# A fixed margin on every handover in the planner of a six-stage perceiver kernel

## The chip, the cores and the metric

The kernel runs on one core of a Trainium2 chip. The metric is device time in microseconds (us) from the start to the end of one execution. TensorE is called PE here, VectorE DVE, ScalarE ACT, GpSimd POOL and SyncE SP; PEld is the weight load of PE. SP does nothing but issue transfers (DMAs).

## What is computed

Two layers work on 128 sequences of 32 tokens with 256 features. Each sequence has a context of 257 tokens. Cut to its steps:

```python
x = x + L0_xattn(layernorm(x), ctx)       # 16 heads of 16; q and k are rms-normed, softmax over 257 keys
x = x + L0_attn(layernorm(x))             # differential attention, 2 heads, 32 keys, rope
x = x + L0_ffn(layernorm(x))              # silu-gated, 704 hidden, weights quantised to NF4 and back
x = x + L1_xattn(layernorm(x), mask, ctx) # 32 heads of 8: masked self attention + tanh(gate) * attention to ctx
x = x + L1_attn(layernorm(x))             # 16 heads, causal
x = x + L1_ffn(layernorm(x))              # 8 gated experts of 256, all computed, weighted by a router
```

## The kernel before

**Units.** Four sequences make a unit of 128 rows, so there are 32 units `h` in each layer. The two feed-forward steps take units in pairs. Numbers that need more than 16 bits are held as a high and a low part (names that end in `l`: `Pl`, `fhl`, `kkl`, `al`): ACT writes or rounds the high part, DVE or POOL subtracts to get the low part, and PE multiplies both.

**Streams.** The work is written as generators, one for each step, and each runs over its units: `ctx_load` and `ctx_gen` (keys and values of the context, written to DRAM), `load_k` and `load_v` (read them back), `A_prep` or `D_prep` (queries), `D_self` (self attention of layer 1), `rowpass` (`khf` and `eh` give a bound `mx` of each row's scores), `pvpass` with `pv` (scores on PE, `P` = exp on ACT, its low part `Pl` on POOL, then values on PE, copied out to `Uc` by ACT), `attn_fin` (division and output projection, into `xt`), `B_gen`, `C_gen`, `E_gen`, `E_att`, and `F_gen` with `F_down` (one expert at a time: `glu_t`, `fhid`, `fhl`, then the product that goes back into `xt`). The weights come through a staging tile `wst`, of which the early ones have a single buffer. `need` and `mark` say which unit of another stream must be emitted first. There are `NX = 8` buffers `xt`: in layer 1, `D_prep(h)` also needs the output of unit `h - 8`.

**The planner.** Every instruction passes through `Eng`, which calls `Est.note`. `Est` keeps a list of busy stretches for each engine. For one instruction, `note` takes the latest time at which its inputs and the place it writes are free, looks for the first gap of its engine after that (`fit`), and books it there for the duration that `cost` gives. A reader on another engine may start at the booked end plus `LAT` of the engine that wrote; so may a reader of SBUF on the same engine. A PSUM bank counts as free at the booked end of its last reader or writer plus `LAT` of that engine. A transfer is booked for 500 ns on SP's queue, then 650 ns and its bytes by 360 to the nanosecond, and then its `LAT`:

```python
for q, (end, by) in self.acc.get(n, {}).items():
    if (w or q[-1] or q[3] == PSB) and self.meet(k, q):
        t = max(t, end if (w or q[3] == PSB) and by == e and e != "dma" else end + self.LAT[by])
...
fin, end = end, end + self.LAT[e]
```

**What the booked times decide.** They decide three things. `Stream.step` sets a stream's key from them, and `pipeline` always steps the live stream with the least key (with 3000 ns in favour of the streams in `HEAVY` while PE has had too few columns in the present stretch of 3413 ns, and 1000 ns against them otherwise). `tk` gives out the one of eight PSUM banks (128x512 numbers) that is free first by these times. And at the end `pipeline` sorts the instructions of each of PE, ACT, DVE, POOL and of SP's queue by their booked start, and pins that order with dependencies that carry no semaphore. The chip knows nothing of the booked times: it runs each engine's list in order, and a list's head waits for its real semaphores.

Of the kernel before, what the change touches and what calls it, by code (L numbers as in the profile page):

```python
# [93 lines left out]
class Est:  # L94


    LAT = {"pe": 196.0, "act": 150.0, "dve": 135.0, "pool": 75.0, "dma": 910.0}

    def __init__(self):
        self.busy = {k: ([], []) for k in ("pe", "act", "dve", "pool", "hw", "dma")}  # L100
# [128 lines left out]
    def note(self, e, op, outs, ins, inst):  # L229
# [3 lines left out]
        for w, L in ((False, R), (True, Wr)):  # L233
            for n, k in L:
# [5 lines left out]
# [3 lines that stand above are left out]
        if e == "dma":  # L243
# [21 lines left out]
        for n, _ in Wr:  # L265
            self.first.setdefault(n, st)
        fin, end = end, end + self.LAT[e]
        for n, k in R:
# [1518 lines left out]
```

## Time and profile before

| | |
|---|---|
| median of three runs | 3359.21 us (3357.96 to 3362.56) |
| profiled execution, device time | 3367.23 us |
| its span, first to last instruction | 3365.5 us, granted clock 0.942 |
| busy: PE, DVE, ACT, POOL | 3002.6, 2433.3, 2249.2, 2137.1 us |
| transfers | 511.64 MB, 152 GB/s |

In the views, a line such as `PE bank L290 <- ACT P L290: 29.0, 50, 2.4` says that PE stood idle 29.0 us in all, 50 times, 2.4 us at the longest, before an instruction that writes a bank, and that the end of an ACT instruction that writes `P` ended the wait. All instructions go through one helper and so bear its line, L290; tiles are told apart by their names. `PE bank` is any matmul, since all of them write a bank. A row of the windows view gives the busy time of each engine in a stretch of the span, with the number of instructions in brackets, then the granted clock of PE and the share of the transfer engines.

### The profile page before, as it was taken

How to read it: one execution, taken by the hardware profiler on the slowest of the kernel's cores; microseconds unless marked ns; L12 is line 12 of the kernel's file. 1: busy time of each engine (PE TensorE's matmuls, PEld its weight loads, DVE VectorE, ACT ScalarE, POOL GpSimd, SP SyncE). 2: the span in 40 equal slices, each digit the busy share in tenths (PEclk: the TensorE clock that was granted, in tenths of full speed). 3: DMA queues.
4: the chain of work that ended last, by engine and by line, in shares of the span. 5: the costliest groups of instructions: out<-in, count | busy, mean ns of one | idle time of the engine just before them, and what ended most of it. 6: DMA issues, size and time to landing. Idle time of an engine off the chain costs nothing. (4 is left out here: it accounts for less than half of the span.)

```text
span 3365.5 us, 106947 instructions
## 1 busy us (share of the span) xinstructions
PE 3002.6 (89%) x41537; PEld 2260.9 (67%) x41537; DVE 2433.3 (72%) x6082; ACT 2249.2 (67%) x6477; POOL 2137.1 (64%) x2546
## 2 busy tenths in 40 slices
PE   3888999999999999999777988988989989999899
PEld 1455767677666677766555766777777777777777
DVE  5786666666666666666576786877887887877876
ACT  2455888787778778876566656656666665666662
POOL 3345777777777777777445656656667565566563
PEclk9889999999999999999677998989999899999999
DMA  3546777777777777776455445445445544444520
GB/s 102 170 133 173 210 210 224 218 216 217 203 216 214 213 217 227 217 210 185 119 150 133 115 100 131 111 107 113 115 115 130 119 113 100 113 113 113 125 57 13
DMA packets 687849, 511.64 MB, mean 152 GB/s; under 512 B 224396, under 2 KB 675340, under 8 KB 687340
## 3 DMA queue, kind: packets, MB, share of 16 engines
q1 hardware_dynamic: 687340, 504.80, 56.2%
q8 instruction: 326, 5.34, 0.7%
q14 instruction: 183, 1.50, 0.2%
HBM read 319.86 MB, written 180.19 MB: 149 GB/s over the span
## 5 line engine op out<-in xcount | busy, mean ns | idle before, releaser
L290 POOL TENSOR_TENSOR Pl<-P 128x512 f16<-128x512 f32 x768 | 806.9, 1066 | 260.6 <-ACT P L290 246.3
L290 ACT ACTIVATE P<-bank 128x512 f32<-128x512 f32 x768 | 439.5, 599 | 89.3 <-PE bank L290 65.9
L290 DVE TENSOR_REDUCE mx<-bank 128x2 f32<-128x512 f32 x768 | 479.4, 681 | 13.3 <-PE bank L290 12.6
L290 ACT COPY Uc<-bank 32x68 f32<-32x68 f32 x1536 | 317.0, 206 | 131.7 <-PE bank L290 108.4
L290 DVE TENSOR_TENSOR vv<-bank,vv 128x256 f16<-128x256 f32 x512 | 214.8, 425 | 149.8 <-ACT vv L290 142.3
L290 POOL TENSOR_TENSOR fhl<-fhid 128x256 f16<-128x256 f32 x256 | 158.0, 617 | 253.1 <-DVE fhid L290 242.8
L290 PE MATMUL bank<-V,P 128*128 128x68 f16 (+1 forms) x4096 | 298.4, 197 | 17.6 <-ACT P L290 5.1
L290 ACT CAST vv<-bank 128x256 f16<-128x256 f32 x512 | 203.3, 403 | 143.4 <-PE bank L290 65.1
L290 PE MATMUL bank<-V,Pl 128*128 128x36 f16 (+1 forms) x3072 | 282.8, 191 | 14.0 <-POOL Pl L290 12.2
L290 PEld LDWEIGHTS <-Kst 128*128 128x128 f16 x4096 | 231.0, 100 | 73.2 <-issue 44.7
L290 PEld LDWEIGHTS <-P 128*128 128x128 bf16 x4096 | 258.5, 101 | 24.5 <-issue 8.2
L290 ACT ACTIVATE glu_t<-bank 128x256 f32<-128x256 f32 x352 | 135.1, 384 | 200.4 <-PE bank L290 181.7
L290 PEld LDWEIGHTS <-Pl 128*128 128x128 f16 x3072 | 236.6, 98 | 46.5 <-POOL Pl L290 20.6
L290 DVE SCALAR_TENSOR_TENSOR glu_t<-glu_t,bank 128x256 f32<-128x256 f32 x352 | 145.4, 413 | 149.8 <-ACT glu_t L290 148.3
L290 PEld LDWEIGHTS <-ch 128*128 128x128 f16 x2048 | 193.2, 99 | 47.0 <-issue 19.1
L290 PE MATMUL bank<-QstD,Kst 128*128 128x128 f16 x2048 | 198.4, 227 | 24.1 <-ACT Uc L290 7.4
L290 POOL TENSOR_TENSOR kk<-kb,kk 128x512 f16<-128x512 f32 x128 | 145.9, 1160 | 100.7 <-ACT kk L290 100.0
L290 PE MATMUL bank<-khf,eh 32*128 32x256 f16 (+1 forms) x1536 | 160.4, 288 | 47.4 <-DVE mx L290 8.7
L290 PEld LDWEIGHTS <-hT 128*128 128x128 f16 x1536 | 136.7, 100 | 94.4 <-issue 15.4
L290 POOL TENSOR_TENSOR cl<-ct,ch 128x1024 f16<-128x1024 f32 x64 | 136.5, 2134 | 21.4 <-ACT ch L290 20.5
L290 DVE SCALAR_TENSOR_TENSOR xt<-bank,w,xt 128x256 f32<-128x256 f32 x256 | 119.6, 472 | 21.1 <-PE bank L290 20.7
L290 PEld LDWEIGHTS <-eh 32*128 32x128 f16 (+1 forms) x1536 | 51.9, 94 | 119.1 <-issue 105.9
(485 smaller groups left out, 9090.2 us busy)
## 6 DMA issues: line engine op xcount, KB each, us to landing
Kst<-kd SPq DMA_DIRECT2D x384, 256.0 KB
kd<-kk SPq DMA_DIRECT2D x128, 512.0 KB
vd<-vv SPq DMA_DIRECT2D x256, 136.0 KB
V<-vd SPq DMA_DIRECT2D x64, 544.0 KB
vd<-vv SPq DMA_DIRECT2D x256, 132.0 KB
V<-vd SPq DMA_DIRECT2D x64, 528.0 KB
ct<-in_ctxm SPq DMA_DIRECT2D x64, 512.0 KB
khf<-kd SPq DMA_DIRECT2D x128, 256.0 KB
```

The costliest lines, as they stand in the source:

```text
L290: r = f(*a, **k)
```

## The change

Each of the five values of `LAT` becomes 150 ns larger. Nothing else is edited: the same instructions with the same operands are emitted, the tile shapes and buffer counts stay, and `cost` stays. What can differ is the order of emission, which bank or buffer a step gets, and the pinned order on each engine and on SP's queue.

```diff
 class Est:
-    LAT = {"pe": 196.0, "act": 150.0, "dve": 135.0, "pool": 75.0, "dma": 910.0}
+    LAT = {"pe": 346.0, "act": 300.0, "dve": 285.0, "pool": 225.0, "dma": 1060.0}
```

## The prediction

> **What bounds the kernel now.** I read the page's busy times first, then the busy times stage by stage, then what PE waits for in the longest stage, then one tile's handovers, and last SP's queue where units change over. The page:
>
> ```profile
> PE 3002.6 (89%) x41537; PEld 2260.9 (67%) x41537; DVE 2433.3 (72%) x6082; ACT 2249.2 (67%) x6477; POOL 2137.1 (64%) x2546
> ```
>
> PE is the fullest engine, and is idle for 3365.5 - 3002.6 = 362.9 us. The windows view, cut where the work changes (start, layer 0, changeover, layer 1, end), says where:
>
> ```profile
> 0.00:360.00 360.00, 262.59 (x2157) 164.33 (x2158) 241.88 (x576) 165.07 (x422) 159.65 (x158) 0.92 0.51 147
> 360.00:1560.00 1200.00, 1158.03 (x13003) 834.43 (x13000) 812.88 (x2069) 961.57 (x2713) 911.63 (x1063) 0.99 0.74 215
> 1560.00:1800.00 240.00, 179.68 (x2141) 127.73 (x2138) 156.34 (x350) 141.97 (x425) 120.91 (x142) 0.74 0.58 149
> 1800.00:3240.00 1440.00, 1290.96 (x22610) 1043.64 (x22608) 1143.69 (x2865) 933.60 (x2782) 887.83 (x1104) 0.94 0.48 113
> ```
>
> The first number after the stretch's length is PE. It is idle 97 us in the start, 42 in layer 0 (3%: PE is the bound there, at clock 0.99), 60 in the changeover and 149 in layer 1 (10%, at clock 0.94). Layer 1 has the most to win or lose. There PE waits mostly for these (us in all, times, longest):
>
> ```profile
> PE bank L290 <- ACT P L290: 21.1, 38, 2.4
> PE bank L290 <- ACT Uc L290: 15.7, 29, 1.9
> PE bank L290 <- DVE mx L290: 12.7, 42, 1.7
> PE bank L290 <- DVE fhid L290: 9.5, 13, 1.7
> PE bank L290 <- POOL Pl L290: 8.4, 16, 1.1
> ```
>
> Nothing on PE reads `Uc` or `mx`: those two rows are banks that come free late. The five rows make 67.4 us in 138 waits, 0.49 us each: many short waits at the head of an ordered list, not one long one.
>
> Most handovers are not tight at all. Of the 768 tiles `Pl`, the tile's view names these waits by PE and PEld:
>
> ```profile
>   PEld L290: 20.6, 41
>   PE bank L290: 13.5, 26
>   PEld bank L290: 4.4, 7
> ```
>
> That is at most 74 waits on 768 tiles; nine tiles in ten lay ready when PE came to them.
>
> Last, SP's timeline at the start of layer 1's steady state:
>
> ```profile
> 1924.56 0.39 SPq L290 DMA_DIRECT2D out_dram<-xt  x1
> ...
> 1926.55 1.63 SPq L290 DMA_DIRECT2D out_dram<-xt  x1
> ...
> 1932.17 0.92 SPq L290 DMA_DIRECT2D xt<-xd  x2
> ```
>
> A pair of units is stored, and 6 us later the pair eight units further on is loaded into the buffers that it left. Layer 1 is a closed loop of eight units: whatever slows one unit from load to store delays the load of another.
>
> **The change part by part.** No instruction is added or taken away, so all terms are waits.
>
> *What is moved on the chip's clock:* nothing. The values that are replaced already describe the chip. `P`: `cost` books 50 + 0.84 x 512 = 480 ns, and 150 makes 630 ns from its start to its reader's; the page's row gives 599 ns for the instruction. `Pl`: 147 + 1.665 x 512 + 75 = 1075 ns, against a row of 1066. So the 150 ns is no correction; it books each reader later than the chip can start it, and puts whatever is ready in between.
>
> *Gain, waits that a margin takes away.* A wait at a list's head goes where the planner now puts other ready work ahead of it. One margin for each of the 138 waits is 138 x 0.15 = 20.7 us in layer 1. The bounds are 0 (no other work was ready) and 67.4 (the margins of two or three handovers add up and cover each wait). I take half of one margin, -10, because two of the five rows wait for a bank, and work put ahead of them needs a bank too.
>
> *Loss, the loop of layer 1.* On the way of a unit from its load to its store I count in the code about 12 handovers in `D_prep`, 7 in `rowpass`, 5 in `pvpass`, 8 in `attn_fin`, 21 in `E_gen` and `E_att`, and 15 in `F_gen` and `F_down` that stand one after another: 68, landings included. Where the planner fills each margin with other work on an ordered engine, that work is really ahead, and the unit really comes later by up to 68 x 0.15 = 10.2 us a trip. 32 units, eight at a time, make 3.75 trips behind one another after the first pair, so at most 38 us; at least 0, if the work put ahead is always done before the data comes. I take 0.6 of it, +23, nearer to the upper end, since a stage in which PE stands idle for 149 us is set in good part by the loop and not by PE.
>
> *Layer 0 and the ends.* In layer 0 PE is 97% busy, so a reader's place is set by what is before it in PE's list rather than by its data: 0, with bounds of -6 (42 us of idle time, at the share of layer 1's gain: 42/149 x 20.7) and +24 (the same loop of eight with some 40 handovers: 4 x 40 x 0.15). In the start each weight chunk goes through one staging buffer from SP to ACT to DVE and back to SP: a chain that no order shortens. PE's longest wait of the kernel, 31.6 us for the chunk of `wa_q`, stands there. Its place in SP's queue could change, which I put at 0, between -15 and +15 (half of it either way). What is queued behind a late landing is all of PE's list.
>
> *SP's queue.* The same 2978 issues in another order. `QstD<-mT`, `Kst<-kd` and the stores of `xt` share it, and each waits for its data at the head. A landing that is booked 150 ns later moves the readers' places, not the issue; it is counted in the 68.
>
> *The clock.* PE's clock in layer 1 is 0.94 although its waits on engines are at most 2.4 us, so short waits cost clock too; at +13 us of idle time on 149 the clock should stay within 0.01, and I add nothing. The Trainium skill's page "TensorE: Matmul & The Clock Gate", under the second failure mode of the clock gate, says that frequent short idle times between groups of matmuls, as banks are cycled, make the clock go back and forth between half and full. That speaks against a change that may scatter matmuls, and the rows' 0.94 beside 0.99 agree with it; an estimate by its half clock is that a drop from 0.94 to 0.93 is 2% more of the stage at half speed, which is 14 us of lost work.
>
> Sum: -10 + 23 = +13 us. Against the profiled execution, 3367.2 + 13 = 3380; that execution lies 8.0 us above the median of the runs, so the forecast against the median is 3359.2 + 13 = **3372 us**.
>
> **The rivals.** About 0.2% (6.7 us) is what a measurement of this kernel can tell from no change.
>
> *A, faster: slack where the list is tight.* Over the whole kernel the same five rows of PE's waits (29.0, 17.7, 27.4, 11.9 and 13.5 us) make 99.5 us in 187 waits. If one margin comes off each and the loop loses nothing, the gain is 187 x 0.15 = 28 us: 3331 us. It decides as soon as more than 23/0.15 = 153 of the waits lose a margin, which pays for the loop's loss as I took it. For it: the waits are short and many. Against it: nine in ten tiles had slack of their own, so most margins go where none was missing. Chance 0.30.
>
> *B, no change: 3359, within 6.7.* Most handovers have more slack than 150 ns, and lists that are full keep their order. For it: the `Pl` view. Against it: the page counts some 59,000 instructions and issues; that many bookings that follow from one another hardly stay in order. Chance 0.13.
>
> *C, much slower.* The whole loop of layer 1 (38) and that of layer 0 (24) come through, with nothing gained: 3359 + 62 = 3421 us. For it: 10% idle time with every engine under 90%. Against it: layer 0 is bound by PE. Chance 0.17.
>
> *The forecast*, some 7 to 40 us slower: 0.40. Its own range is 3366 to 3399.
>
> **How the numbers follow.** Slower takes in the forecast and C: 0.57. Same is B, 0.13; faster is A, 0.30. The range runs from just beyond A's price, 3328, to somewhat short of C's, 3416, which leaves a part of A (more than one margin for each wait) and of C outside, about 0.2 together. It is wide, with both signs in it, since the sum is small against its own terms.
>
> **What would show it.** Right: the busy times of all engines are unchanged within some us; PE's idle time in layer 1 is above 149 us by 10 to 25; the rows `<- ACT P`, `<- ACT Uc` and `<- DVE mx` are shorter, and waits at places where the unit's chain goes through (`hT`, `dPT`, `tr`, `QstD<-ed`) are longer; the stores of `xt` in layer 1 come further apart than now. Wrong: the idle time falls in layer 1 with the loop's pace, which is A; or the time moves in the start or the changeover by more than 15 us, which is a place in SP's queue and no handover; or PE's busy time moves by more than 20 us at a clock other than 0.94, so that the throttle decides and not the waits.

## The result, and the profile after

| | before | with the margin |
|---|---|---|
| median of five runs | 3362.56 us | 3383.33 us |
| ratio to before, 95% interval | | 1.0059, 1.0041 to 1.0076 |
| span of the profiled execution | 3365.5 us | 3383.6 us |
| granted clock, mean | 0.942 | 0.938 |

The kernel is 0.59% slower, 20.8 us between the medians; the forecast was 13 us. No engine has more to do: the counts of instructions are those of before. The page's busy line after the change:

```profile
PE 3004.5 (89%) x41537; PEld 2261.9 (67%) x41537; DVE 2444.5 (72%) x6082; ACT 2230.1 (66%) x6477; POOL 2130.7 (63%) x2546
```

PE's busy time is 1.9 us up, the span 18.1, so over the whole kernel nearly all of the difference is idle time of PE. By stages it is not, as shown below. The windows view, with the same cuts as before:

```profile
0.00:360.00 360.00, 262.67 (x2275) 168.04 (x2276) 257.47 (x603) 174.29 (x456) 170.59 (x173) 0.95 0.55 156
360.00:1560.00 1200.00, 1150.97 (x13037) 832.53 (x13035) 802.77 (x2060) 954.47 (x2715) 909.46 (x1061) 0.99 0.74 214
1560.00:1800.00 240.00, 179.08 (x2353) 124.32 (x2353) 163.85 (x360) 140.35 (x419) 119.03 (x134) 0.76 0.58 144
1800.00:3240.00 1440.00, 1284.55 (x21929) 1033.13 (x21928) 1125.13 (x2802) 902.95 (x2717) 867.03 (x1092) 0.92 0.47 111
```

Layer 1 is the row that became worse: clock 0.92 where it was 0.94, and 21,929 matmuls done in the stretch where it was 22,610. Cut by stores of units on SP's queue instead of by time, the start and layer 0 together end at 1692 us, 18 us sooner than before; from there to the first stored pair of layer 1 is 210 us (217 before); to the 28th stored unit 1363 us (1330); and the last four units take 119 us (108). So the change gains 25 us ahead of the first stored pair and loses 44 behind it. Some of both is work that only moved: 193 matmuls more lie behind that store with the change, some 12 us at the pace of layer 1 (an estimate from 20,876 matmuls in 1330 us).

From the first stored pair to the 28th unit PE does nearly the same number of matmuls (20,867, before 20,876), so these 33 us can be taken apart. PE's idle time is 11.0 us longer (146.0, before 135.0) and its busy time 21.7 us (1217.1, before 1195.4), while the time at half clock went from 163.8 to 218.4 us. (The clock's records hold only 1 and 0.5.) In the start and layer 0 it is the other way round: 99.0 us at half clock, 133.1 before, and 19.1 us less busy time for 36 matmuls more. The two stages cancel in the page's busy line.

What PE waits for from 1800 to 3240 us, with the change:

```profile
PE bank L290 <- DVE fhid L290: 32.0, 19, 6.0
PE bank L290 <- DVE mx L290: 22.4, 48, 4.0
PE bank L290 <- DMA QstD<-ed: 16.0, 4, 5.4
...
PE bank L290 <- ACT P L290: 12.1, 27, 1.7
PE bank L290 <- ACT Uc L290: 8.9, 18, 1.3
PE bank L290 <- POOL Pl L290: 7.8, 19, 0.9
```

Three of the five rows that the prediction went by have shrunk (`ACT P` from 21.1, `ACT Uc` from 15.7, `POOL Pl` from 8.4 us). The two that are DVE's have grown, and with few long waits: `DVE fhid` from 9.5 us (1.7 at the longest) to 32.0 (6.0). From the first stored pair to the 28th unit, waits of PE over 2 us went from 10 with 29.0 us to 17 with 58.6 us, while those of 0.6 to 2 us fell from 64.9 to 47.7 us.

**One of the long waits.** PE's timeline after the change has this:

```profile
2031.75 0.37 PE L290 MATMUL bank<-khf,eh 32*128 32x256 f16 x2 [0.26 <-ACT aT L290]
2038.08 0.58 PE L290 MATMUL bank<-khf,eh 32*128 32x256 f16 x2 [5.96 <-DVE fhid L290]
```

`rowpass` wants a bank that an expert's product fills; DVE empties it when it computes `glu_t` and `fhid`. DVE's timeline over the same microseconds shows where DVE was:

```profile
2027.37 0.23 DVE L290 TENSOR_SCALAR z<-bank,temp 128x16 f32<-128x16 f32 x1 [0.17 <-PE bank L290]
...
2029.97 0.97 DVE L290 SCALAR_TENSOR_TENSOR zn<-inh,zn 128x16 f32<-128x16 f32 x1
...
2033.99 0.17 DVE L290 TENSOR_REDUCE m<-eq 128x2 f32<-128x16 f32 x1
2034.19 0.17 DVE L290 TENSOR_TENSOR eq<-eq,m 128x16 f32<-128x16 f32 x1
2034.40 0.17 DVE L290 TENSOR_TENSOR eq<-eq,eq 128x16 f32<-128x16 f32 x1
...
2037.06 0.17 DVE L290 TENSOR_TENSOR w<-w,ws 128x16 f32<-128x16 f32 x1
2037.16 0.42 DVE L290 SCALAR_TENSOR_TENSOR glu_t<-glu_t,bank 128x256 f32<-128x256 f32 x1
2037.61 0.42 DVE L290 TENSOR_TENSOR fhid<-glu_t,bank 128x256 f32<-128x256 f32 x1
```

From behind `z` to the last `w` lies the router of the experts: 34 instructions on DVE, most of which read what the one before wrote in SBUF, most of them 0.17 us long and 0.2 us apart. ACT had finished `glu_t` at 2030.5; the two evictions stood in DVE's list behind the whole chain until 2037.16, and PE stood still. The chain is there before the change too, one for each of the 16 pairs. What is new is its place in the plan, because a reader of SBUF on the same engine also pays `LAT`: the margin makes the planner think that the chain takes 34 x 0.15 = 5.1 us longer. How that turns into waits of 6 us on the chip was not followed step by step.

The chain is also longer on the chip. From `z` to the last `w`, the 16 chains take 160.2 us in all with the change, 132.5 before. Of their instructions 56 take 0.4 us or more, 42.6 us together, where it was 28 with 22.9 us; over nine tenths of the time of each, POOL is running, as here (`zn` above took 0.97 us):

```profile
2027.86 4.04 POOL L290 TENSOR_TENSOR Pl<-P 128x512 f16<-128x512 f32 x4
```

The 16 chains take 156 to 173 us in the four kernels whose pinned order of layer 1 has 150 or 152 ns on reads by the same engine and the router in one block (the change and e3, e5, e7 below), and 131 to 136 us in the kernel before, e1, e2, e6 and e9. But their length alone does not set the time: e6 has the shortest chains and is the slowest kernel of all.

A measure for all runs follows from this: PE's idle time, and the time at half clock, in the 16 us after each `z`, summed over the 16 routers. Some of the expectations below take the end of each chain as the limit instead (idle stretches that end up to 1.5 us behind it, each in full): 29.8 us before, 56.0 with the change.

### The profile page after: what moved, and what is told of

Read it like the earlier page. It is cut to its first block, busy times and chain, and to the rows that moved or that the text cites. A ratio compares the mean times of both kernels' runs of the same rounds, so it can differ in the third digit from the quotient of the medians.

```text
span 3383.6 us, 106895 instructions
## 1 busy us (share of the span) xinstructions
PE 3004.5 (89%) x41537; PEld 2261.9 (67%) x41537; DVE 2444.5 (72%) x6082; ACT 2230.1 (66%) x6477; POOL 2130.7 (63%) x2546
## 4 chain that ended last, share of the span: by engine, by line
PE 58%; DVE 18%; DMA 9%; ACT 7%; issue 4%; POOL 3%; SPq 1%; DVEq 0%; ACTq 0%; POOLq 0%
PE bank L290 58%; DVE mx L290 4%; POOL Pl L290 1%; DMA QstD<-ed 1%; SPq L290 1%; DVE dS L290 1%; DVE nfmk L290 1%; ACT P L290 1%; ACT Uc L290 1%; DMA QstA<-mT 1%; DMA khf<-kd 1%; DVE vv L290 1%; DVE rbt L290 1%; DVE eq L290 1%; ACT vv L290 1%
## 5 line engine op out<-in xcount | busy, mean ns | idle before, releaser
L290 PE MATMUL bank<-V,P 128*128 128x68 f16 (+1 forms) x4096 | 299.6, 196 | 19.1 <-DVE fhid L290 5.9
L290 ACT CAST vv<-bank 128x256 f16<-128x256 f32 x512 | 203.8, 403 | 146.0 <-PE bank L290 78.9
L290 PE MATMUL bank<-khf,eh 32*128 32x256 f16 (+1 forms) x1536 | 176.2, 289 | 73.7 <-DVE fhid L290 18.6
```

What stands on the lines that cost most here:

```text
L290: r = f(*a, **k)
```

## The experiments

Each ratio is to the kernel before on the same chip.

| kernel | ratio, 95% interval | idle after `z` | at half clock after `z` |
|---|---|---|---|
| before | 1 | 42.6 us | 60.8 us |
| the change, 150 ns | 1.0059, 1.0041 to 1.0076 | 65.9 | 105.9 |
| e1, 2 ns | 1.0086, 1.0062 to 1.0110 | 51.6 | 78.3 |
| e2, 150 ns up to 1500 us | 1.0086, 1.0060 to 1.0112 | 60.0 | 90.9 |
| e3, 150 ns from 1500 us | 1.0036, 1.0020 to 1.0052 | 44.5 | 79.1 |
| e4, 300 ns | 0.9966, 0.9950 to 0.9983 | 39.4 | 50.2 |
| e5, pinned order of 150 ns alone | 1.0170, 1.0150 to 1.0190 | 56.2 | 78.3 |
| e6, emission of 150 ns alone | 1.0309, 1.0289 to 1.0328 | 67.2 | 119.8 |
| e7, 152 ns | 1.0053, 1.0038 to 1.0068 | 55.3 | 96.5 |
| e8, 302 ns | 0.9967, 0.9952 to 0.9982 | 24.6 | 46.7 |
| e9, 150 ns, not on reads by the same engine | 1.0009, 0.9993 to 1.0026 | 52.7 | 67.9 |
| e10, 300 ns on DVE's own reads alone | 1.0061, 1.0041 to 1.0081 | 40.8 | 63.3 |
| e11, router as a stream, no margin | 0.9995, 0.9981 to 1.0009 | 23.7 | 16.9 |
| e12, router as a stream, 150 ns | 0.9926, 0.9906 to 0.9946 | 15.7 | 12.1 |

**The size of the margin, and where it lies (e1 to e4).** The theory of the prediction was the loop: each margin that is filled with other work really delays the unit, so the loss grows with the margin and lies in layer 1. The rival was a lottery: any new order of lists as long as these is a new draw. For e1 and e4 the five values of `LAT` are 2 and 300 ns larger than before; for e2 and e3:

```diff
+    def lat(self, e, t):
+        return self.LAT[e] + (150.0 if t < 1.5e6 else 0.0)      # e3: t >= 1.5e6
...
-        ... end + self.LAT[by])
+        ... end + self.lat(by, end))
-        fin, end = end, end + self.LAT[e]
+        fin, end = end, end + self.lat(e, end)
```

> A margin of 2 ns in place of 150: far below any handover, but it can reorder the lists. Loop theory (each margin filled with other work really delays the unit, so the loss grows with the margin): within 0.1% of before, 3 us at most. Lottery theory (any new order of the lists is worse or better by chance, whatever the margin): it moves the time as much as the 150 ns did, some 10 to 25 us either way.

> The 150 ns only where the booked end lies before 1500 us of the plan, which is the start and layer 0. The profile of the change stores layer 0's last unit 18 us earlier and layer 1's first pair 26 us earlier than before. Loop theory: layer 0 keeps that lead and layer 1 runs at the old pace, so 15 to 26 us faster than before, about 3340 us. Lottery theory: layer 1's lists come out anew as well, so anything within 25 us of before.

> The 150 ns only where the booked end lies at or after 1500 us of the plan, which is the changeover, layer 1 and the end. In the profile of the change the first to the last pair of outputs of layer 1 lie some 40 us further apart than before. Loop theory: 35 to 45 us slower than before, more than the full change. Lottery theory: anything within 25 us of before.

> A margin of 300 ns everywhere. Loop theory: twice the loss of the 150 ns, some 35 to 50 us slower than before, with the loss in layer 1 (70 to 90 us there, less a lead of layer 0). Lottery theory: not slower than with 150 ns in particular, within 25 us of before either way.

The loop theory misses all four. 2 ns cost 0.86%, more than 150; 300 ns gain 0.34%; the margin in the first half alone costs 0.86%, though its layer 1 is planned without any. The lottery's 25 us are left too, by e1 and e2 with 27 and 29 us between the medians. So the mere order of the lists is worth up to 0.9% here, and no single run tells a mechanism by its time. e2 also shows what one list does by itself: its lists are the change's up to one instruction on ACT, which started at 1537.69 us in the one profile and at 1544.94 in the other. Of the 18 us by which the change's profile led at the end of layer 0, some 7 may be of that kind.

**Emission or pinned order (e5, e6), and the neighbours (e7, e8).** In e5 and e6 a second `Est` is kept beside the first. The first decides whose turn it is and which bank and buffer a step gets; the pinned order is sorted from the second:

```diff
-        self.est = Est()
+        self.est = Est(0.0, Est(150.0))          # e6: Est(150.0, Est(0.0))
...
     def note(self, e, op, outs, ins, inst):
+        if self.shadow:
+            self.shadow.note(e, op, outs, ins, inst)
...
-        for L in [est.log[k] for k in PIN]:
+        for L in [est.shadow.log[k] for k in PIN]:
```

> The streams are stepped, and banks and buffers given out, by a plan without margin, exactly as before; a second plan with 150 ns is kept beside it, and only the pinned order of each engine and of SP's queue comes from that one. Theory of slack (what matters is the pinned order round the handovers): like the full change, 15 to 25 us slower than before. Theory of emission (what matters is which unit comes first and which bank it gets): within 7 us of before. Lottery theory: neither, anywhere from 15 us faster to 30 us slower.

> The other half: streams, banks and buffers by the plan with 150 ns, and the pinned order from a second plan without margin. Theory of slack: within 7 us of before. Theory of emission: 15 to 25 us slower than before, like the full change. Lottery theory: anywhere from 15 us faster to 30 us slower.

> 152 ns in place of 150. If the size of the margin decides, this is the full change again: 15 to 25 us slower than before. Lottery theory: a new draw, which may lie 15 us or more from the 150 ns.

> 302 ns in place of 300, which was 11 us faster than before. If a margin of that size is good by itself (it takes the short waits away): 5 to 17 us faster than before again. Lottery theory: a new draw, on average some 10 to 20 us slower than before.

Neither half carries the change: both are far slower than the whole, 1.7% and 3.1%, and outside every range that was expected. In both, an order that is pinned by other times than those by which turns and banks were given out is worse than either plan used throughout. The neighbours came out as the size of the margin would have it. The lists for 152 ns part from those for 150 within the first 100 us, and the time is the same again (1.0053 beside 1.0059); 302 agrees with 300 (0.9967 beside 0.9966). Their stretches after `z` agree too: 96.5 and 105.9 us at half clock, against 46.7 and 50.2. This speaks against the lottery as the only cause, but weakly: a third pair of neighbours, 0 and 2 ns, lies 0.86% apart, so two pairs that agree may be chance.

One thing that differs between the two pairs is the router. With 300 ns the planner leaves 435 ns between two of its instructions, and an eviction of 256 columns (booked at 334 ns as `fhid`, 392 as `glu_t`) fits into such a gap; with 285 ns it does not, as it did not with 135. DVE's timeline of e8:

```profile
2025.04 0.15 DVE L290 SCALAR_TENSOR_TENSOR zn<-inh,zn 128x16 f32<-128x16 f32 x1
2025.39 0.42 DVE L290 SCALAR_TENSOR_TENSOR glu_t<-glu_t,bank 128x256 f32<-128x256 f32 x1 [0.20 <-ACT glu_t L290]
2025.74 0.18 DVE L290 TENSOR_TENSOR w<-w,zn 128x16 f32<-128x16 f32 x1
...
2026.26 0.17 DVE L290 TENSOR_TENSOR eq<-eq,const 128x16 f32<-128x16 f32 x1
2026.36 0.41 DVE L290 TENSOR_TENSOR fhid<-glu_t,bank 128x256 f32<-128x256 f32 x1
2026.69 0.16 DVE L290 TENSOR_REDUCE m<-eq 128x2 f32<-128x16 f32 x1
```

Here the first expert's bank is emptied in the midst of the chain. Over the 16 routers the longest unbroken run of router instructions is 29.2 on average before, 24.4 with the change, 6.6 in e4 and 8.3 in e8, and 15 to 16 other instructions stand between them, where there were 2 to 3. Of the 16 evictions `glu_t` and `fhid` of a pair, about eight lie inside the chain in e4 and e8, and next to none before and with the change.

**The router alone (e9 to e12).** The new theory: what 150 ns lose, they lose in the router's stretches, by the reads on the same engine. Against it still the lottery. e9 takes the margin from every read on the same engine, not from the router's alone. In e11 and e12 `F_gen` also waits for the router of the pair before (not shown in the diff).

```diff
 # e9, with the five values of the change
-        ... and by == e and e != "dma" else end + self.LAT[by])
+        ... and by == e and e != "dma" else end + self.LAT[by] - (150.0 if by == e != "dma" else 0.0))
 # e10, with the values of before
+        ... and by == e and e != "dma" else end + self.LAT[by] + (300.0 if by == e == "dve" else 0.0))
 # e11, with the values of before; e12, with those of the change
-    def router(self, hT):
+    def router(self, g):
+        yield from self.need(("hT", g))
...
         nc.vector.tensor_scalar(inh, inh, 1.0, None, ALU.add)
+        yield [inh]                     # and so after each instruction
...
-        w = self.router(hT)             # in F_gen
+        self.hTF[g] = hT
...
-        yield from self.need(("Fu", n))             # in F_down
+        yield from self.need(("Fu", n), ("R", g))
```

> 150 ns on every handover between engines and every landing, but not on a read of SBUF by the engine that wrote it (so the planner's chain of small router instructions on DVE keeps its old length). Router theory (the change loses in the 16 stretches in which DVE runs the router's 34 small instructions as one block, with the banks' evictions behind them; PE idles 29.8 us there before, 56.0 with the change): PE's idle time there falls back to 25 to 42 us, and the time comes to at most 10 us above before. Lottery theory: no link between the two; the time 5 to 30 us above before, the router stretches anything.

> 300 ns more only where DVE reads from SBUF what DVE wrote; every other value as before. In the plan the gaps between two router instructions then are 435 ns, wide enough for an eviction of 256 columns (planned at 334 to 392 ns). Router theory: the block is broken up as with 300 and 302 ns everywhere (longest unbroken run 7 to 8 of 34 there, 29 before), PE's idle time in the router stretches stays under 33 us, and the time is 5 to 15 us under before. Lottery theory: 5 to 30 us above before.

> No margin; the router becomes a stream of its own that yields after each instruction, so that others are booked between them, and F_down waits for its weights by name. Router theory: the block is broken up without any margin, PE's idle time in the router stretches is under 30 us, and the time is 5 to 20 us under before. Lottery theory: 5 to 30 us above before.

> The router as a stream of its own, and the 150 ns of the change everywhere. Router theory: the 26 us that the change lost in the router stretches come back, so 15 to 35 us faster than the change, which is from 15 us under before to 5 above. Lottery theory: as the change, 5 to 30 us above before.

*e9* came out as the router theory said, by both numbers: no difference from before, and 32.3 us of idle time to the end of the chains. All handovers between engines and all landings carry the 150 ns there. The 16 chains take 132.9 us, as before the change (132.5). In the 16 us after each `z` PE idles 52.7 us, which is between before and the change. Its row of the windows view for layer 1, and the two grown rows of its waits:

```profile
1800.00:3240.00 1440.00, 1294.69 (x22232) 1044.71 (x22233) 1136.45 (x2834) 918.08 (x2744) 869.47 (x1088) 0.93 0.47 112
```

```profile
PE bank L290 <- DVE fhid L290: 24.2, 19, 4.5
PE bank L290 <- DVE mx L290: 22.2, 69, 2.7
```

The clock is back to 0.93, but DVE's rows are not back to 9.5 and 12.7 us: the waits on `mx` and part of those on `fhid` come with the margin between engines.

*e12* is the fastest kernel of the study, 3337.75 us beside 3363.13, 45 us below the change by the two ratios (0.0133 x 3363). More than the 26 us that I expected to come back did, so it is not those alone. Its waits in layer 1 have the `fhid` row of before the change or less, and the end of the kernel runs at full clock:

```profile
PE bank L290 <- DVE fhid L290: 6.0, 8, 2.5
```

```profile
1800.00:3240.00 1440.00, 1296.07 (x22659) 1051.62 (x22657) 1165.89 (x2847) 940.05 (x2831) 902.71 (x1128) 0.93 0.47 113
3240.00:3400.00 160.00, 91.40 (x1292) 79.20 (x1289) 70.96 (x217) 26.62 (x74) 33.56 (x55) 1.00 0.04 9
```

Its last four units take 79 us, against 119 with the change and 108 before. That is mostly work done earlier: 891 matmuls are left at that point, against 1535 and 1333. PE's idle time there is 5.9 us, against 15.5 and 12.9.

*e11 and e10* missed. In e11 the router's stretches lose least but for e12 (23.7 and 16.9 us), and its last four units take 74 us (719 matmuls); yet its time is that of before, since the first pair of layer 1 is stored 31 us later (1958 against 1927) and half clock turns up elsewhere (422.8 us in all, 394.4 before). My expected 30 us of idle time to the end of the chains was also a poor measure there: a chain that others may enter lasts 29.7 us instead of 8.3, and 73.2 us of idle time fall into it. In e10 the chain is broken up less than foreseen (longest run 11.4), PE idles as little as foreseen (29.6 us), and the kernel is slower all the same, with 459.8 us at half clock. So a broken chain is not enough by itself. Nor do the stretches after `z` stand for the whole of layer 1: from 1800 to 3240 us, e4 and e8 spend 230 and 220 us at half clock, hardly less than the change (232) and more than before (187), and are faster than both.

## Why the prediction was right or wrong

**Sign and size** were right: 13 us forecast, 20.8 measured. But the sum reached it by a wrong term and with the clock's at nothing, so that it came out so near is luck. PE's idle time from 1800 to 3240 us rose from 149.0 to 155.5 us, less than the 10 to 25 us that were to show the forecast right.

**The gain** was put at -10 us for layer 1, half a margin for each of 138 short waits. Where PE waits on ACT or POOL it is there: the three rows fell from 45.2 to 28.8 us, 16.4 less. The reservation made at that step (rows that wait for a bank are not helped) holds for `mx`, which rose by 9.7 us, and not for `Uc`, which fell by 6.8. Of the check list, `<- DVE mx` getting shorter was wrong.

**The loop**, +23 us, is the step that failed. It priced the margin as a delay of each unit that grows with it. 300 ns were faster than none, e2 and e3 did not keep to their halves, and the places where the waits of a delayed unit should have shown mostly did not grow: of DVE's tiles, `hT` went from 8.4 to 4.9 us, `dPT` from 5.1 to 0.4 and `tr` stayed at 2.4, and only `QstD<-ed` rose, from 10.0 to 16.0. A unit's way from load to store did become longer, by 9.6 us on average for the 9th to the 28th (403.8 to 413.4), but with eight in flight any loss of pace does that, and with 300 ns it is 404.1. What the runs showed in its place is a loss that gathers at the one chain that the count of 68 handovers left out, since it crosses hardly any engine: the router on DVE, with 23.3 us more idle time of PE and 45.1 us more at half clock in the stretches after `z`. I had read the line of `note` that pads a read on the same engine and gave it no term. That the chain causes this loss is argued, not shown (see below).

**The clock** was put at 0, with 0.01 as the most that it should move. In the stretch from 1800 to 3240 us it went from 0.935 to 0.919, and the time at half clock from 187 to 232 us: 45 us more, worth up to 23 us of work. All of it lies in the router's stretches: in that stretch they have 53.1 us at half clock before and 97.7 with the change, and the rest has 133.5 and 134.4. From the first stored pair to the 28th unit PE was busy 21.7 us longer for as many matmuls, twice as much as it was idle longer, with 54.6 us more at half clock. So what goes with this term, which the sum put at nothing, is the larger part of what that stretch lost, though not strictly: e4 has 215.0 us at half clock there, and PE was busy 1208.2 us for 20,807 matmuls. The premise was also misread: PE's waits on engines in layer 1 are not 2.4 us at most, which holds for the five rows shown, but 3.3 (`ka`), 3.2 (`hT`) and 2.8 (`dPT`). What the prediction cites from the Trainium skill's page "TensorE: Matmul & The Clock Gate" (the second failure mode) agrees in direction with these rows. The estimate beside it, 14 us for 0.01, would be 23 us for the 0.016 measured. Across the kernels of the table, idle time and half clock after `z` mostly go together, but not strictly: e8 and e11 idle 24.6 and 23.7 us there, and have 46.7 and 16.9 us at half clock.

**Layer 0 and the changeover** were put at 0 and came out 25 us sooner in the profile. By the windows most of the lead at the end of layer 0 is the start's, within its bound of 15 us: 118 matmuls more by 360 us and only 34 more in layer 0's stretch, some 11 and 3 us at layer 0's pace of 10.8 matmuls per us (an estimate). Two executions of the same lists differ there by 7.

**Rival B** held for the tiles that it was argued from: waits on `Pl` are 53 and 31 of 768 with the change, 41 and 26 before. It failed on the order, which was new from the first 100 us on. **Rival A** may be right about what the margin between engines does at its best: e9 has it without a loss and e12 with a gain, though a new order of lists could give either.

**What stays open.** The order alone moves the time by up to 0.9% (e1). e9 lies 0.5% under the change, which such a draw could also give; that the router is the cause rests on its stretches, where the change's extra half clock lies and which go along with the margin in e4, e7, e8 and e9, on the fall from the change to e12, and on the agreement of two pairs of neighbours, not on one time. Against it stand the third pair, e11, which has far less half clock after `z` than the kernel before and no gain, and the half clock of e4 and e8 over all of layer 1. Whether the banks come late by the plan's longer booking or by POOL's work that falls under the chain was not separated. Why 2 ns cost 0.86%, and why e10 is slow with a chain that is broken up, was not found.

## What to carry to other kernels

A list scheduler that books a long chain of tiny dependent instructions in one go closes that engine's list to everything behind it: look at what evicts a PSUM bank behind such a chain, and try to let other work be booked between them. Here that alone gained nothing (e11), and together with the margin 0.7% (e12). A margin in a planner acts wherever its latency is read, reads on the same engine included, and it acts by thresholds (what fits into a gap), not in proportion. Before a change of order is explained, run a control that changes nothing but the draw (2 ns here): its 0.9% is the least that a time alone must show, and below it a measure taken at the place in question is needed as well. And a busy time that is unchanged over a whole kernel can hide two stages whose clocks moved against each other: cut it at points of equal work.

## What the runs showed of the hardware

- From the end of the releaser to the start of the waiting instruction, the median in the trace of before goes by the engine that waits: 33 to 39 ns into ACT and DVE, 51 to 55 into PE, 77 to 79 into POOL from ACT or DVE (56 from PE).
- Dependent instructions of at most 16 columns on DVE start 0.2 us apart at 0.17 us each, but 28 of those in the routers' chains before the change took 0.41 to 1.06 us, each with POOL running for over nine tenths of it. Not every one beside POOL is longer: 61 others lay for more than half of their time beside a running POOL instruction and took under 0.4 us.
- Between the same two stores of layer 1, 20,867 matmuls kept PE busy for 1217.1 us with 218.4 us at half clock; before the change, 20,876 for 1195.4 us with 163.8.
- The same lists, run twice, lay 7.3 us apart after 1540 us (the change and e2), in layer 0, where PE is 97% busy.
